# A selective scan with one product moved to GpSimd, and a Toeplitz matrix laid over 128 rows, in an eight-sublayer kernel

## The chip, the core and the metric

The kernel runs on one NeuronCore of a Trainium2 chip. Its engines are TensorE (PE; its weight loads are shown as PEld), VectorE (DVE), ScalarE (ACT), GpSimd (POOL) and SyncE (SP), which here only issues DMAs. Each engine works through its own row of instructions in order; rows wait for each other by semaphores. The metric is device time of the whole kernel in microseconds (us). A run is one execution; a time is a median of runs.

## The reference, cut to what matters

The kernel computes two layers of four sublayers each. Only two sublayers are touched. Sublayer A is a complex-valued recurrence over 2048 positions, for 2 batches, 256 channels (D) and 16 states (N):

```
c_mag(z)   = sqrt(re^2 + im^2 + 1e-8)
c_phase(z) = arctan2(im, re + 1e-10)
def step(h, inp):
    x_t, dt_t, B_t, C_t, xr_t = inp
    h_carrier = h.mean(axis=1)
    T = cos((c_phase(xr_t) - c_phase(h_carrier)) / 2) ** 2
    alpha = exp(dt_t[..., None] * A_neg)
    expo = 1 + (1 - alpha) * 0.5 * (1 - T[:, None, :])
    mag, ph = c_mag(h), c_phase(h)
    h = from_polar(min(exp(expo * log(mag + 1e-8)), 10), ph)
    h = h + B_t * (dt_t * x_t)
    h = from_polar(tanh(c_mag(h)), c_phase(h))
    y_t = einsum('bnc,bdnc->bd', C_t, h)
```

Each step needs the state of the step before, and the mean of that state over the channels. The 1e-10 in `c_phase` and the 1e-8 in `c_mag` are kept by the kernel as first-order terms.

Sublayer C, on an input of 2 x 2048 positions x 256 features:

```
x, z = split(W_in @ hidden)               # 512 channels each
x = silu(causal convolution of x with 4 taps + bias)
y = irfft(rfft(x, 2L) * rfft(k_ssm, 2L))[..., :L]   # causal, k_ssm is [512, 1024]
y = (y + x * D_skip) * silu(z)
out = W_out @ y
```

## The kernel before, in words

`tile_hybrid_kernel` (L1607) runs the sublayers one after the other: sublayer A (`scan_tables`, L159, then `scan`, L257, then an output projection), a router, sublayer B, a router, sublayer C (L1073), and then the second layer's feed-forward and attention parts (`feed_forward`, L1273, and `sublayer_d`, L1394).

**The scan.** `scan_tables` prepares, for all positions, the tables that a step needs; its `softplus` helper on VectorE ends in L254 (two SBUF tiles multiplied, 128x512), and L217 multiplies two 128x512 tiles on GpSimd. L205 copies a PSUM tile on VectorE. In `scan`, the 128 partitions are 2 batches x 16 states x 4 groups of channels, and each partition holds 64 channels (J). A state has a real and an imaginary part, so an operation that is made for both (`for k2 in range(2)`) is two instructions. `step` (L400 to L489) writes one time step; 16 steps (TG) form a group with its own tables, 32 groups form one round of the hardware loop at L514, which goes round four times: 2048 steps. Inside the loop the order of every engine's row is the order of the Python text (`manual_schedule()` at L516): no scheduler moves anything. The step goes so:

- TensorE, L410: the means `hc` and `hd` of the state, from the sums `hs` that the step before has left.
- VectorE: `gl` (L414) from `lg` of the step before, `dot` (L420), `ex` (L424) from `kd` of the step before, `ngd` (L425).
- ScalarE: `sq` (L418), `ln` (L427), `ci` (L428), `ea` = exp of `ex` (L429), `fac` (L439), and then, in `act_gap`, work for the next step or group (L391, L385).
- VectorE: `p` from the old state and `ea` (L436, L437), times `fac` (L442), plus the drive `bx` (L444), then `z`, `q`, `m2`, `r1` (L446 to L454), and `dve_gap`.
- ScalarE, L459 to L473, twelve activations that take logarithms and exponentials: `lm`, `lr`, `m`, `ir`, `e`, `rm` (inverse magnitude), `le`, `ld`, `sg`, `lb`, `k1`, `k2c`. Of these `lm`, `m`, `lr`, `le` and `lb` are PSUM tiles (`wa(...)`); the rest are in SBUF.
- VectorE, the end of the step: `p` times `ir` (L475), times e - 1 (L477), then

```
V.scalar_tensor_tensor(dl, p[:, 0], 0.5 * SMALL, rm, ALU.mult, ALU.mult)        # L480
V.tensor_tensor_reduce(out=hn[:, k2], in0=p[:, k2], in1=sg, ..., accum_out=hs)  # L482, twice
V.tensor_tensor(th, ld, le, ALU.subtract)                                       # L486
V.scalar_tensor_tensor(kc, k2c, 2.0 * MAG_EPS, k1, ALU.mult, ALU.add)           # L487
V.scalar_tensor_tensor(lg[o], th, 2.0, kc, ALU.mult, ALU.add)                   # L488
V.scalar_tensor_tensor(kd[o], kc, 0.5, dl, ALU.mult, ALU.add)                   # L489
```

L482 writes the new state into `hist` and its sum over the channels into `hs`, for which TensorE waits at L410. `dl` is the 1e-10 term (SMALL is 1e-10, MAG_EPS 1e-8). `lg`, `kd` and `hs` have two buffers each, one for odd and one for even steps. `project` (L491) multiplies the finished state with C on TensorE, one step late. GpSimd has no work in the scan. L357 and L358 make the first `kd`, once.

**Sublayer C.** 512 channels are four blocks `e` of 128; the positions are 16 blocks of 128 for each batch. The long convolution of one channel is a product with a Toeplitz matrix of its 1024 kernel values. `kernels` (L1102) loads one tile `toep` of 128 partitions x 4 x 1216: row p of it is the reversed, zero-padded kernel of a channel (`C_krev`, 1280 values to a channel) shifted by p. Each half of 64 rows belongs to four other channels, so a tile serves 8 channels. Two DMAs fill it, one issued by SyncE (r = 0) and one by ScalarE (r = 1); three buffers (`kb`). `convolve` (L1162) multiplies with it: 9 block distances `m` x 2 halves `h` x 4 channels `j` x 2 row halves `r` = 144 matmuls of 64 rows x 32 weight columns x 128 columns, into two PSUM tiles `ps[r]`, in groups that four tiles share. After four tiles `leave` (L1177) copies the two on ScalarE (L1181) and stores them to `c_yd` by ScalarE's queue.

Around this, the block `e + 1` is made and the block `e - 1` is finished in portions of 512 positions: `produce` (L1123; projection, taps of the short convolution on VectorE at L1139, SiLU `xs` on ScalarE at L1141, a store by GpSimd's queue), `turn` (L1145; 16 matmuls that transpose `xs` in halves of 64, and two copies into `xring`), `finish` (L1187; two loads by GpSimd's queue, skip and gate) and `project` (L1202; the output product). The loop at L1224 takes 16 tiles for each `e`, 64 in all, a portion every second tile. Here only TensorE's row is in the order of the text (`manual_schedule` of PE, L1120); the other rows are ordered by the scheduler. At the head of the sublayer, `norm_transpose` (L119) normalizes and transposes its input. `feed_forward` and its neighbours have no part in the change; the prediction takes the price of an instruction from L1268 (VectorE, 128x2048), L1322, L1374, L1376 and L1556 (GpSimd and VectorE products).

Of the kernel before, what the change touches and what calls it, by code (L numbers as in the profile page):

```python
# [17 lines left out]
AF = mybir.ActivationFunctionType  # L18
ALU = mybir.AluOpType
# [4 lines left out]
P = 128  # L24
B, S, D = 2, 2048, 256
NT = B * S
NI = NT // P
NB = S // P
# [9 lines left out]
SMALL = 1e-10  # L38
MAG_EPS = 1e-8
# [8 lines left out]
L_CONV = 1024  # L48
TOEP = L_CONV + P
KREV = 1280  # L50
# [3 lines left out]
HALF = P // 2  # L54
# [5 lines left out]
def new(pool, shape, name, **kw):  # L60
    return pool.tile(list(shape), F32, name=name, tag=name, **kw)


class Kernel:
# [192 lines left out]
    def scan(self, y, dtd, dxd, tabd):  # L257
# [6 lines left out]
        tc, nc = self.tc, self.nc  # L264
        V, A, G = nc.vector, nc.scalar, nc.gpsimd
        J, TURN = 64, TG * GROUPS
        with ExitStack() as c:
# [51 lines left out]
            with nc.allow_non_contiguous_dma(reason="short vectors"):  # L319
                for b in range(B):  # L320
                    rows = slice(b * 64, (b + 1) * 64)
# [78 lines left out]
            def step(k, g, before, act_gap, dve_gap):  # L400
# [61 lines left out]
                ir, e, sg, rm, ld = (w([J], n) for n in ("ir", "e", "sg", "rm", "ld"))  # L462
                A.activation(ir, lr, AF.Exp, scale=-0.5)  # L463
                A.activation(e, m, AF.Exp, scale=-2.0)
                A.activation(rm, lm, AF.Exp, scale=-1.0)
                le = wa("m")
                A.activation(le, e, AF.Ln, bias=1.0)
                A.activation(ld, e, AF.Ln, scale=-1.0, bias=1.0)
                A.activation(sg, le, AF.Exp, scale=-1.0)  # L469
                lb, k1, k2c = wa("lr"), w([J], "k1"), w([J], "k2c")  # L470
                A.activation(lb, m2, AF.Ln, bias=MAG_EPS)
                A.activation(k1, rm, AF.Ln, scale=MAG_EPS, bias=1.0)
                A.activation(k2c, lb, AF.Exp, scale=-0.5)  # L473
                for k2 in range(2):
                    V.tensor_tensor(p[:, k2], p[:, k2], ir, ALU.mult)  # L475
                for k2 in range(2):
                    V.scalar_tensor_tensor(p[:, k2], e, -1.0, p[:, k2], ALU.add, ALU.mult)  # L477
                th, kc, dl = (w([J], n) for n in ("th", "kc", "dl"))

                V.scalar_tensor_tensor(dl, p[:, 0], 0.5 * SMALL, rm, ALU.mult, ALU.mult)  # L480
                for k2 in range(2):
                    V.tensor_tensor_reduce(  # L482
                        out=hn[:, k2], in0=p[:, k2], in1=sg, scale=-1.0, scalar=0.0 if k2 else J * SMALL,
                        op0=ALU.mult, op1=ALU.add, accum_out=hs[o][:, k2 : k2 + 1],
                    )
                V.tensor_tensor(th, ld, le, ALU.subtract)  # L486
                V.scalar_tensor_tensor(kc, k2c, 2.0 * MAG_EPS, k1, ALU.mult, ALU.add)  # L487
                V.scalar_tensor_tensor(lg[o], th, 2.0, kc, ALU.mult, ALU.add)  # L488
                V.scalar_tensor_tensor(kd[o], kc, 0.5, dl, ALU.mult, ALU.add)  # L489

            def project(g, k, yps):  # L491

# [580 lines left out]
    def sublayer_c(self):  # L1073
# [11 lines left out]
        with ExitStack() as c:  # L1085
# [10 lines left out]
            xring = [new(kp, [P, HALF, 2, TAPS + NB, B], f"c_x{j}") for j in range(2)]  # L1096
            for t in xring:
                G.memset(t[:, :, :, 0:TAPS], 0.0)
# [12 lines left out]

            with tc.tile_pool(name="c_ln", bufs=2) as lp, tc.tile_pool(name="c_pl", bufs=2, space=PSUM) as pl:
# [10 lines left out]
            def produce(e, ch):  # L1123

                b, i0, cs = ch // 4, ch % 4 * 4, slice(ch * CH, (ch + 1) * CH)
                ps = new(pp, [P, CH], "ps")
                for k in range(2):
                    nc.tensor.matmul(ps, wi[:, k, e * P : (e + 1) * P], xT[:, k, cs], start=k == 0, stop=k == 1)
                xin = new(xp, [P, 3 + CH], "c_xi")
                if i0 == 0:  # L1130
                    V.memset(xin[:, 0:3], 0.0)
                else:
                    V.tensor_copy(xin[:, 0:3], last[0][:, CH : CH + 3])
                A.copy(xin[:, 3:], ps)
                last[0] = xin
                acc = new(tp, [P, CH], "c_acc")
                V.tensor_scalar(acc, xin[:, 0:CH], cw[:, e, 0:1], cb[:, e : e + 1], ALU.mult, ALU.add)
                for j in range(1, 4):
                    V.scalar_tensor_tensor(acc, xin[:, j : j + CH], cw[:, e, j : j + 1], acc, ALU.mult, ALU.add)  # L1139
                xs = new(tp, [P, CH], "c_xs")  # L1140
                A.activation(xs, acc, AF.Silu)  # L1141
                G.dma_start(out=xd[e * P : (e + 1) * P, cs], in_=xs)
                return e, ch, xs

            def turn(e, ch, xs):  # L1145

                b, i0 = ch // 4, ch % 4 * 4
                ps = new(pt, [P, 2, 4, HALF], "ps_t")
                for h in range(2):
                    for j in range(4):  # L1150
                        for r in range(2):
                            rows = slice(r * HALF, (r + 1) * HALF)
                            lo = j * P + h * HALF
                            nc.tensor.matmul(
                                ps[rows, h, j, :], xs[:, lo : lo + HALF], self.ident[:, rows], start=True, stop=True
                            )
                for h in range(2):
                    V.tensor_copy(
                        xring[e % 2][:, :, h, TAPS + i0 : TAPS + i0 + 4, b], ps[:, h].rearrange("p j c -> p c j")
                    )  # L1160

            def convolve(e, g, t, ps):  # L1162
                x = xring[e % 2]
                for m in range(TAPS + 1):
                    for h in range(2):
                        lo = L_CONV - m * P + h * HALF
                        for j in range(4):
                            for r in range(2):
                                rows = slice(r * HALF, (r + 1) * HALF)
                                nc.tensor.matmul(  # L1170
                                    ps[r][j * 32 : (j + 1) * 32, g % 4, :],
                                    x[rows, 4 * g + j, h, TAPS - m : TAPS - m + NB, :].rearrange("p i b -> p (i b)"),
                                    t[rows, j, lo : lo + P],
                                    start=m == 0 and h == 0, stop=m == TAPS and h == 1,
                                )

            def leave(e, g, ps):  # L1177

                for r in range(2):
                    ys = new(tp, [P, 4, P], "c_ys")  # L1180
                    A.copy(ys, ps[r][:, :, ::-1])  # L1181
                    rows = slice(e * P + r * HALF + 4 * g, e * P + r * HALF + 4 * g + 16)
                    A.dma_start(
                        out=yd[rows].rearrange("(s j) i b t -> (j i b) s t", j=4), in_=ys
                    )

            def finish(e, ch):  # L1187
                b, i0, cs = ch // 4, ch % 4 * 4, slice(ch * CH, (ch + 1) * CH)
# [33 lines left out]
                later(turn, t)  # L1222
            later(turn)
            for e in range(E):  # L1224
                for g in range(HALF // 4):
                    t = kernels(e, g)
                    if g % 4 == 0:
                        ps = [new(pc, [P, 4, P], f"ps_c{r}") for r in range(2)]
                    convolve(e, g, t, ps)
                    if g % 4 == 3:  # L1230
                        leave(e, g - 3, ps)
                    if g % 2 == 0:
                        work = []
                        if e + 1 < E:
                            work.append((turn, produce(e + 1, g // 2)))
                        if e > 0:
                            work.append((project, finish(e - 1, g // 2)))
# [469 lines left out]
```

## Time and profile before

| what | before |
|---|---|
| median of 3 runs | 14147.37 us (14145.97 to 14152.4) |
| the profiled execution | 14151.41 us |
| its span | 14149.7 us |
| instructions | 282029 |
| mean granted TensorE clock | 0.61 |
| busy: TensorE | 5571.1 us (39%) |
| busy: weight loads | 3830.2 us (27%) |
| busy: VectorE | 10378.9 us (73%) |
| busy: ScalarE | 8647.8 us (61%) |
| busy: GpSimd | 415.6 us (3%) |
| head of sublayer A, 0 to 310 us | GpSimd busy 24.7 us |
| the scan, 310 to 10169 us | VectorE busy 8322.7 us, ScalarE 7255.6, TensorE 2274.1, GpSimd 0 |
| sublayer C, 11095 to 12254 us | TensorE busy 694.7 us, VectorE 262.9, ScalarE 96.6; DMA share 0.70 |

How to read the profile. "Slices": the span is cut in 40 equal parts of 354 us; a digit is the busy share of an engine in tenths. "Groups": one row for a line and an engine, with the operation, out <- in by tile names, sizes, the number of instructions (x), then the busy sum in us and the mean length in ns, then the engine's idle time just before these instructions and what ended most of it. "Timeline": start in us, length in us, engine, line, operation and tiles of each instruction; lengths of instructions that follow each other overlap, so what an instruction costs its row is the spacing of starts, not its length. "Windows": a stretch, its length, the busy time and number of instructions of PE, PEld, DVE, ACT and POOL, then the granted TensorE clock, the DMA share and GB/s. "Waits": tile and line, what was waited for, then the summed us, the number of waits and the mean us of one. "Loads": a DMA's tiles, its queue, number, KB of one, and median us from issue to landing. "issue" is idle time for which the profile shows no event.

### The profile page before, as it was taken

The page shows a single profiled execution, that of the slowest core. Times are in us where ns is not written, and L with a number is a line of the kernel's source. Part 1 is how long each engine was busy: PE and PEld are TensorE (multiplying, and loading weights), DVE is VectorE, ACT ScalarE, POOL GpSimd, SP SyncE. Part 2 cuts the span into 40 slices and gives each one's busy share as a digit, 9 for nine tenths or more (in the row PEclk, how much of TensorE's full clock was granted, in tenths as well). Part 3 has the DMA queues.
Part 4 walks back from the last instruction along what each step waited for, and adds up shares of the span by engine and source line. Part 5 has one row for each costly group of instructions (what it writes and reads, how often), then busy time and mean ns, then how long its engine had stood idle before and what let it go on. Part 6 is the DMA issues. An engine that isn't in the chain of part 4 may idle for free. (4 is left out here: it accounts for less than half of the span.)

```text
span 14149.7 us, 282029 instructions
## 1 busy us (share of the span) xinstructions
PE 5571.1 (39%) x76456; PEld 3830.2 (27%) x76456; DVE 10378.9 (73%) x65267; ACT 8647.8 (61%) x44978; POOL 415.6 (3%) x496
## 2 busy tenths in 40 slices
PE   4222222222222222222222222222389655778888
PEld 2111111111111111111111111111255444544445
DVE  6888888888888888888888888888757411355555
ACT  3777777777777777777777777777535100234444
POOL 0000000000000000000000000000000000031110
PEclk6555555555555555555555555555579787889999
DMA  3000000000000000000000000000000477342220
GB/s 79 14 17 14 17 15 15 17 14 17 16 14 17 14 17 17 14 17 14 17 17 14 17 14 17 17 14 17 10 13 1 105 186 187 86 99 34 34 33 20
DMA packets 349182, 461.08 MB, mean 33 GB/s; under 512 B 205026, under 2 KB 245033, under 8 KB 346548
## 3 DMA queue, kind: packets, MB, share of 16 engines
q1 hardware_dynamic: 296372, 319.91, 10.0%
q10 hardware_dynamic: 36352, 88.61, 2.6%
q0 software_dynamic: 14848, 34.36, 0.9%
q8 instruction: 611, 10.01, 0.3%
q14 instruction: 999, 8.18, 0.2%
HBM read 385.55 MB, written 52.46 MB: 31 GB/s over the span
## 5 line engine op out<-in xcount | busy, mean ns | idle before, releaser
L410 PE MATMUL hc<-hs,mean 128*32 128x2 f32 x16384 | 588.4, 203 | 7238.6 <-DVE hs L482 7174.4
L410 PEld LDWEIGHTS hc<-hs,mean 128*32 128x32 f32 x16384 | 413.0, 140 | 7450.7 <-DVE hs L482 7386.1
L475 DVE TENSOR_TENSOR p<-p,ir 128x64 f32<-128x64 f32 x4096 | 739.6, 222 | 1063.8 <-ACT ir L463 1063.8
L494 PE MATMUL yps<-cs,hist 128*64 128x8 f32 x8192 | 1225.0, 259 | 13.4 <-DVE hs L482 13.4
L459 ACT ACTIVATE lm<-m 128x64 f32<-128x64 f32 x2048 | 466.3, 228 | 1217.1 <-DVE m L451 1217.1
L391 ACT ACTIVATE bx<-dx,tc 128x64 f32<-128x64 f32 x4098 | 1170.7, 333 | 0.1
L418 ACT ACTIVATE sq<-hc 128x2 f32<-128x2 f32 x2048 | 352.6, 172 | 1169.7 <-PE hc L410 1169.7
L1531 ACT ACTIVATE d_p<-ps_e 128x512 f32<-128x512 f32 (+3 forms) x1280 | 599.6, 537 | 755.4 <-PE ps_o L1512 532.0
L494 PEld LDWEIGHTS yps<-cs,hist 128*64 128x64 f32 x8192 | 1033.3, 218 | 45.5 <-DVE hs L482 13.8
L482 DVE CUSTOM_DVE_ANT_0 hist<-p,sg 128x64 f32<-128x64 f32 x4096 | 751.5, 220 | 11.9 <-DVE hs L482 6.0
L442 DVE TENSOR_TENSOR p<-p,fac 128x64 f32<-128x64 f32 x4096 | 741.7, 222 | 8.9 <-DVE p L437 6.5
L477 DVE SCALAR_TENSOR_TENSOR p<-e,p 128x64 f32<-128x64 f32 x4096 | 739.6, 222 | 9.9 <-ACT sg L469 9.2
L444 DVE TENSOR_TENSOR p<-p,bx 128x64 f32<-128x64 f32 x4096 | 726.9, 219 | 2.5
L439 ACT ACTIVATE fac<-ngd,ci 128x64 f32<-128x64 f32 x2048 | 712.7, 348 | 1.0 <-DVE p L436 1.0
L436 DVE SCALAR_TENSOR_TENSOR p<-hist,ea 128x64 f32<-128x64 f32 x2048 | 462.0, 226 | 323.2 <-ACT ea L429 323.2
L1524 PE MATMUL ps_e<-d_qt,d_kt 128*128 128x512 f32 (+3 forms) x1280 | 556.4, 444 | 45.7 <-ACT d_p L1531 36.4
L410 PE MATMUL hd<-hs,mean 128*32 128x2 f32 x16384 | 545.2, 193 | 0.0
L429 ACT ACTIVATE ea<-ex 128x64 f32<-128x64 f32 x2048 | 525.6, 257 | 24.4 <-DVE ex L424 5.2
L1481 PE MATMUL ps_m<-d_kt,d_qt 128*128 128x512 f32 (+3 forms) x1280 | 498.9, 436 | 98.5 <-DVE d_part L1486 38.8
L1170 PE MATMUL ps_c<-toep,c_x 64*32 64x128 f32 x18432 | 383.4, 320 | 385.2 <-issue 384.1
L432 PE MATMUL hd<-ident,ci 128*1 128x1 f32 x4096 | 386.7, 163 | 354.3 <-ACT ci L428 346.8
L1491 DVE TENSOR_REDUCE d_part<-ps_m 128x1 f32<-128x512 f32 x768 | 495.0, 684 | 41.6 <-PE ps_m L1481 40.7
(448 smaller groups left out, 22020.5 us busy)
## 6 DMA issues: line engine op xcount, KB each, us to landing
toep<-in_C_krev ACTq DMA_DIRECT2D x64, 1216.0 KB, 14.0
toep<-in_C_krev SPq DMA_DIRECT2D x64, 1216.0 KB, 9.8
ng<-dtd SPq DMA_DIRECT2D x258, 256.0 KB, 3.7
dx<-dxd SPq DMA_DIRECT2D x258, 256.0 KB, 4.2
d_kt<-d_kd SPq DMA_DIRECT2D x128, 128.0 KB, 4.3
d_qt<-d_qd SPq DMA_DIRECT2D x128, 128.0 KB, 3.9
y<-ys SPq DMA_DIRECT2D x512, 8.0 KB, 1.9
c_xd<-c_xs POOLq DMA_DIRECT2D x32, 256.0 KB, 6.6
```

Of the source, the lines that this page charges most:

```text
L391: A.activation(bx[o][:, k2], tg[j][2][:, k], AF.Identity, scale=tg[j][0][:, k2, k : k + 1], bias=0.0 if k2 else SMALL,)
L410: nc.tensor.matmul(out[r : r + 32], mean[:, r : r + 32], hs[i], start=True, stop=True)
L429: A.activation(ea, ex, AF.Exp)
L439: A.activation(fac, ngd, AF.Exp, scale=ci)
L442: V.tensor_tensor(p[:, k2], p[:, k2], fac, ALU.mult)
L444: V.tensor_tensor(p[:, k2], p[:, k2], bx[o][:, k2], ALU.add)
L475: V.tensor_tensor(p[:, k2], p[:, k2], ir, ALU.mult)
L477: V.scalar_tensor_tensor(p[:, k2], e, -1.0, p[:, k2], ALU.add, ALU.mult)
L482: V.tensor_tensor_reduce(out=hn[:, k2], in0=p[:, k2], in1=sg, scale=-1.0, scalar=0.0 if k2 else J * SMALL, op0=ALU.mult, op1=ALU.add, accu ...
L494: nc.tensor.matmul(yps[:, k, :], hist[g][:, k, k2], tg[g][3][:, k2, k], start=k2 == 0, stop=k2 == 1)
L1524: nc.tensor.matmul(s[:, q0:], ks[kt // 4][:, hh, kt % 4 * P : (kt % 4 + 1) * P], q[:, hh, q0:], start=True, stop=not diag,)
L1531: A.activation(pr[:, q0:], s[:, q0:], AF.Exp, scale=0.25)
```

## The change

In the scan, the product `dl` leaves VectorE for GpSimd and reads the new state in place of the old `p`: it no longer holds the factor 0.5e-10, and it is made after the two instructions of L482. The factor goes to the `scalar_tensor_tensor` that makes `kd`. `kd` is kept doubled, and `ex` takes half of it: a `tensor_tensor` becomes a `scalar_tensor_tensor`. The twelve activations of ScalarE get another order, in which `lb` comes sixth, `rm` eighth (ahead of `sg`), `ld` and `k1` last; `lb` gets a PSUM tile of its own.

In sublayer C, a tile `toep` now serves 4 channels, whose shifted kernels stand over all 128 rows. Row 64 + p of a channel is row p shifted by 64 further values, so only half of the tile is loaded: SyncE's DMA loads the upper 64 rows of two channels, ScalarE's the lower 64 rows of the other two (608 KB each), and the missing halves are copied on the chip, one by VectorE and one by ScalarE. `low` and `up` are the lower and the upper rows; the second two channels are held at another offset, for which `lo` makes up. There are 128 tiles instead of 64, 36 matmuls of 128 rows for each instead of 144 of 64 rows, one PSUM tile for four of them, four transposes and one copy in `turn`. A portion of `produce` and `finish` comes every fourth tile.

```
@@ scan, before the loop
-            V.scalar_tensor_tensor(n1, first[:, 0], -SMALL, n1, ALU.mult, ALU.mult)
-            V.scalar_tensor_tensor(kd[1], n2h, 0.5, n1, ALU.mult, ALU.add)
+            V.scalar_tensor_tensor(n1, first[:, 0], -2.0 * SMALL, n1, ALU.mult, ALU.mult)
+            V.tensor_tensor(kd[1], n2h, n1, ALU.add)
@@ step
-                V.tensor_tensor(ex, kd[i], gl, ALU.subtract)
+                V.scalar_tensor_tensor(ex, kd[i], 0.5, gl, ALU.mult, ALU.subtract)
...
-                A.activation(rm, lm, AF.Exp, scale=-1.0)
+                lb, k1, k2c = wa("lb"), w([J], "k1"), w([J], "k2c")
+                A.activation(lb, m2, AF.Ln, bias=MAG_EPS)
                 le = wa("m")
                 A.activation(le, e, AF.Ln, bias=1.0)
+                A.activation(rm, lm, AF.Exp, scale=-1.0)
+                A.activation(sg, le, AF.Exp, scale=-1.0)
+                A.activation(k2c, lb, AF.Exp, scale=-0.5)
                 A.activation(ld, e, AF.Ln, scale=-1.0, bias=1.0)
-                A.activation(sg, le, AF.Exp, scale=-1.0)
-                lb, k1, k2c = wa("lr"), w([J], "k1"), w([J], "k2c")
-                A.activation(lb, m2, AF.Ln, bias=MAG_EPS)
                 A.activation(k1, rm, AF.Ln, scale=MAG_EPS, bias=1.0)
-                A.activation(k2c, lb, AF.Exp, scale=-0.5)
...
-                V.scalar_tensor_tensor(dl, p[:, 0], 0.5 * SMALL, rm, ALU.mult, ALU.mult)
                 for k2 in range(2):
                     V.tensor_tensor_reduce(
...
+                G.tensor_tensor(dl, hn[:, 0], rm, ALU.mult)
                 V.tensor_tensor(th, ld, le, ALU.subtract)
                 V.scalar_tensor_tensor(kc, k2c, 2.0 * MAG_EPS, k1, ALU.mult, ALU.add)
                 V.scalar_tensor_tensor(lg[o], th, 2.0, kc, ALU.mult, ALU.add)
-                V.scalar_tensor_tensor(kd[o], kc, 0.5, dl, ALU.mult, ALU.add)
+                V.scalar_tensor_tensor(kd[o], dl, -2.0 * SMALL, kc, ALU.mult, ALU.add)
@@ sublayer_c, kernels
                 t = new(kb, [P, 4, W], "toep")
+                up, low = t[0:HALF], t[HALF:P]
                 for r in range(2):
-                    first = kr.offset + (e * P + r * HALF + 4 * g) * KREV
+                    first = kr.offset + (e * P + 4 * g + 2 * r) * KREV
                     (nc.scalar if r else nc.sync).dma_start(
-                        out=t[r * HALF : (r + 1) * HALF],
-                        in_=bass.AP(kr.tensor, first, [[1, HALF], [KREV, 4], [1, W]]),
+                        out=(low if r else up)[:, 2 * r : 2 * r + 2],
+                        in_=bass.AP(kr.tensor, first, [[1, HALF], [KREV, 2], [1, W]]),
                     )
+                V.tensor_copy(low[:, 0:2, 0 : W - HALF], up[:, 0:2, HALF:W])
+                A.copy(up[:, 2:4, HALF:W], low[:, 2:4, 0 : W - HALF])
@@ turn
+                for j in range(4):
+                    nc.tensor.transpose(ps[:, j, :], xs[:, j * P : (j + 1) * P], self.ident)
+                V.tensor_copy(
+                    xring[e % 2][:, :, TAPS + i0 : TAPS + i0 + 4, b], ps.rearrange("p j c -> p c j")
+                )
@@ convolve
+                    for j in range(4):
+                        lo = L_CONV - m * P + j // 2 * HALF
+                        nc.tensor.matmul(
+                            ps[j * 32 : (j + 1) * 32, g % 4, :],
+                            x[:, 4 * g + j, TAPS - m : TAPS - m + NB, :].rearrange("p i b -> p (i b)"),
+                            t[:, j, lo : lo + P], start=m == 0, stop=m == TAPS,
+                        )
@@ leave
+                ys = new(tp, [P, 4, P], "c_ys")
+                A.copy(ys, ps[:, :, ::-1])
+                rows = slice(e * P + 4 * g, e * P + 4 * g + 16)
+                A.dma_start(out=yd[rows].rearrange("(s j) i b t -> (j i b) s t", j=4), in_=ys)
@@ the loop
-                for g in range(HALF // 4):
+                for g in range(P // 4):
...
-                    if g % 2 == 0:
+                    if g % 4 == 0:
...
-                    else:
+                    elif g % 4 == 2:
```

More of the change, by code (lines that the diff above doesn't have):

```diff
@@ L1095, in sublayer_c @@
             dk = self.load_cols(kp, "C_D_skip")
-            xring = [new(kp, [P, HALF, 2, TAPS + NB, B], f"c_x{j}") for j in range(2)]
+            xring = [new(kp, [P, P, TAPS + NB, B], f"c_x{j}") for j in range(2)]
             for t in xring:
-                G.memset(t[:, :, :, 0:TAPS], 0.0)
+                G.memset(t[:, :, 0:TAPS], 0.0)
             kb = c.enter_context(tc.tile_pool(name="c_kb", bufs=3))
@@ L1147, in turn @@
                 b, i0 = ch // 4, ch % 4 * 4
[L1148 to L1160, printed above, removed]
+                ps = new(pt, [P, 4, P], "ps_t")
+                for j in range(4):
[3 more added lines that the diff above has]
+                )
             def convolve(e, g, t, ps):
@@ L1164, in convolve @@
                 for m in range(TAPS + 1):
[L1165 to L1175, printed above, removed]
-            def leave(e, g, ps):
[L1179 to L1185, printed above, removed]
+                    for j in range(4):
[5 more added lines that the diff above has]
+                        )
+            def leave(e, g, ps):
+                ys = new(tp, [P, 4, P], "c_ys")
+                A.copy(ys, ps[:, :, ::-1])
+                rows = slice(e * P + 4 * g, e * P + 4 * g + 16)
+                A.dma_start(out=yd[rows].rearrange("(s j) i b t -> (j i b) s t", j=4), in_=ys)
             def finish(e, ch):
@@ L1224, in sublayer_c @@
             for e in range(E):
-                for g in range(HALF // 4):
+                for g in range(P // 4):
                     t = kernels(e, g)
                     if g % 4 == 0:
-                        ps = [new(pc, [P, 4, P], f"ps_c{r}") for r in range(2)]
+                        ps = new(pc, [P, 4, P], "ps_c")
                     convolve(e, g, t, ps)
@@ L1231, in sublayer_c @@
                         leave(e, g - 3, ps)
-                    if g % 2 == 0:
+                    if g % 4 == 0:
                         work = []
                         if e + 1 < E:
-                            work.append((turn, produce(e + 1, g // 2)))
+                            work.append((turn, produce(e + 1, g // 4)))
                         if e > 0:
-                            work.append((project, finish(e - 1, g // 2)))
-                    else:
+                            work.append((project, finish(e - 1, g // 4)))
+                    elif g % 4 == 2:
                         for f, args in work:
```

## The prediction, made before the changed kernel was run

> **What bounds the kernel now.** I read the page first (engine rows by slice, costliest groups), then VectorE's timeline over one step of the scan, then the waits, windows and loads of the Toeplitz stage.
>
> ```profile
> DVE  6888888888888888888888888888757411355555
> DMA  3000000000000000000000000000000477342220
> L410 PE MATMUL hc<-hs,mean 128*32 128x2 f32 x16384 | 588.4, 203 | 7238.6 <-DVE hs L482 7174.4
> L475 DVE TENSOR_TENSOR p<-p,ir 128x64 f32<-128x64 f32 x4096 | 739.6, 222 | 1063.8 <-ACT ir L463 1063.8
> ```
>
> Slices 2 to 28 look alike: the 2048 dependent scan steps, from 363.6 us (first L414) to 10175.2 us (last L489), so 4.79 us each. TensorE idles for the sums of L482, VectorE for L463: no engine is full, and a step is one loop of dependences, mostly VectorE's. The Toeplitz loop runs from 11171.0 to 12170.2 us, where the DMA digit is 7. One step's end on VectorE (start, length):
>
> ```profile
> 5007.05 0.36 DVE L477 SCALAR_TENSOR_TENSOR p<-e,p 128x64 f32<-128x64 f32 x2
> 5007.38 0.23 DVE L480 SCALAR_TENSOR_TENSOR dl<-p,rm 128x64 f32<-128x64 f32 x1
> 5007.53 0.22 DVE L482 CUSTOM_DVE_ANT_0 hist<-p,sg 128x64 f32<-128x64 f32 x1
> 5007.67 0.08 DVE L482 DVE_READ_ACCUMULATOR2_ANT hs<- 128x1 f32 x1
> 5007.67 0.22 DVE L482 CUSTOM_DVE_ANT_0 hist<-p,sg 128x64 f32<-128x64 f32 x1
> ...
> 5007.81 0.22 DVE L486 TENSOR_TENSOR th<-ld,m 128x64 f32<-128x64 f32 x1
> 5007.95 0.22 DVE L487 SCALAR_TENSOR_TENSOR kc<-k2c,k 128x64 f32<-128x64 f32 x1
> 5008.20 0.23 DVE L488 SCALAR_TENSOR_TENSOR lg<-th,kc 128x64 f32<-128x64 f32 x1
> 5008.34 0.22 DVE L489 SCALAR_TENSOR_TENSOR kd<-kc,dl 128x64 f32<-128x64 f32 x1
> ```
>
> There is no gap from L480 to L489, and the chain runs on through gl, ex, ngd (L414 to L425) to ScalarE's exponentials. So dl costs the step its whole spacing, 0.143 us (0.15 in this rounding).
>
> **The scan, part by part.** Count from the first hist of a step, T0.
>
> Gain: without dl on VectorE, hist follows L477. It also needs sg. ScalarE keeps sg ninth in its row, so sg still ends at 7.35 in this step; dl starts at 7.38, and hist can start there. Everything behind it moves up 0.143 us: 2048 x 0.143 = 293 us.
>
> ScalarE's new order: ld and k1 now come last, k2c earlier. Logarithms follow each other at 0.15 us and exponentials at 0.11, so k1, last, ends near 7.75, and ld near 7.60. th would start at 7.67 and kc at 7.81: no wait, with some 0.05 us to spare. Were a tenth of a microsecond missing, it would cost 205 us; I take nothing. lb now has its own PSUM tile: nothing. rm's new wait is on a GpSimd product two steps old: nothing. L424 and L489 keep one VectorE instruction each (226 and 218 ns before; scalar_tensor_tensor rows cost 218 to 226): nothing. L357/L358 run once.
>
> Added: dl on GpSimd, and kd's wait for it. The trace has no such product in the scan; its nearest rows (mean ns behind the comma):
>
> ```profile
> L1556 POOL TENSOR_TENSOR d_on<-d_on,d_rc 128x512 f32<-128x512 f32 x32 | 40.9, 1277 | 65.5 <-DMA d_rc<-d_sd 65.5
> L1322 POOL TENSOR_TENSOR d_half<-d_rot,d_half 128x1024 fp32r<-128x1024 f32 x16 | 37.9, 2370 | 18.5 <-ACT d_half L1321 17.3 <-DMA d_qd<-d_half 1.2
> L217 POOL TENSOR_TENSOR sa_dx<-sa_dt,sa_xin 128x512 f32<-128x512 f32 x16 | 22.8, 1422 | 266.9 <-DVE sa_dt L255 266.9
> ```
>
> From 1277 and 2370 a line of 2.13 ns an element over 0.18 us: 64 elements take 0.32 us. hist's accumulator read ends at T0+0.23; GpSimd starts 0.08 us after VectorE's end where it waits for it (L1376 behind L1374, six times 79 to 87 ns). So dl runs from T0+0.31 to T0+0.63. kd stood at T0+0.81: its own wait is covered by 0.15 us.
>
> But L217 shows two lengths, 1.27 and 1.58 us, and its neighbour on VectorE stretches with it:
>
> ```profile
> 79.71 1.58 POOL L217 TENSOR_TENSOR sa_dx<-sa_dt,sa_xin 128x512 f32<-128x512 f32 x1 [22.00 <-DVE sa_dt L255]
> 80.20 1.64 DVE L254 SCALAR_TENSOR_TENSOR sp_a<-sp_a,sp_s 128x512 f32<-128x512 f32 x1
> ```
>
> L254 takes 0.69 us alone (its fastest eight), 1.16 or 1.64 beside L217: it really starts at 81.84 - 0.69 = 81.15, 0.14 us before L217's end at 81.29. L205 and L1374, with one input in PSUM, do not stretch. kc (L487) reads two SBUF tiles and would start at T0+0.42; th reads one from PSUM. By this row kc may start at T0+0.63-0.14 = 0.49, 0.065 us late, and lg, kd, gl, ex, ngd queue behind it. Net 0.143 - 0.065 = 0.078 us a step, 160 us. The Trainium skill ("SBUF — State Buffer", section "SBUF: two separate sides") is harsher: a VectorE instruction with two SBUF inputs and a reading GpSimd instruction hold the shared port pair exclusively, and the loser blocks for the whole instruction. Then kc waits until 0.63, 0.21 us late, and the step grows by 0.06 us: +130 us. The row is of this chip and of this pair of instructions, so I take the row. Ends: 0 late (-293 us) to 0.21 late (+130 us).
>
> **The Toeplitz stage.** Views: windows, waits, loads.
>
> ```profile
> 11171.00:12171.00 1000.00, 596.72 (x19579) 450.73 (x19580) 151.17 (x262) 60.20 (x103) 45.23 (x74) 0.80 0.75 182
> PE ps_c L1170 <- issue: 384.1, 86, 6.7
> toep<-in_C_krev ACTq DMA_DIRECT2D x64, 1216.0 KB, 14.0
> toep<-in_C_krev SPq DMA_DIRECT2D x64, 1216.0 KB, 9.8
> ```
>
> DMA share is 0.75 at 182 GB/s; TensorE waits 384 us for "issue", in stalls of about 6 us, not for data. Each tile's two loads start when TensorE has finished a tile (11357.18, 11372.42), they move one after the other (9.8 and 14.0 us to land), and while they move TensorE, after some 160 records at 16 ns, waits for more instructions. One tile (8 channels) takes 15.6 us, 16 channels 31.2 us.
>
> Removed: half the matmuls (18432 records to 9216), so half their instructions; the 6 us stalls should mostly go. Not removed: bytes. 128 tiles with two loads of 608 KB are the same 159 MB, whose floor at 182/0.75 = 243 GB/s is 656 us. Added: 128 copies of 2304 elements on each of VectorE and ScalarE. VectorE: 128x2048 in 1.27 us (L1268), so 1.4 us, beside idle time. ScalarE: 0.22 us at 64 and 0.59 at 512 elements, so 2.1 us. That copy stands in the queue that issues half of the loads. In the built program ScalarE's row over four tiles is: load 9, ys copy, load 10, ys store, xi copy, copy 9, (silu), copy 10, xs, load 11, load 12, copy 11, copy 12. Each copy holds up the next load; before, loads only waited for a buffer.
>
> Chain, from the end of copy 8: the packet records give 1.4 us from issue to the first packet, 2.8 us for 608 KB (2.49 MB in 11 us before) and 1.0 us to the semaphore, in order of arrival. Load 9 lands at 5.2; SP's 10 at 8.0; ScalarE's 10, issued at 1.2 behind ys, at 10.8; SP's 11 at 13.6. Copy 9 ends at 7.6, copy 10 at 12.9. xs waits for VectorE's taps (L1139), queued behind its copy 11: it ends at 17.7. Loads 11 and 12 follow, land at 23.4 and 26.2; copy 12 ends at 28.3. For e = 0 load 11 precedes xs: 26.9. The x and y traffic, 1 MB per 16 channels, is 4.6 us of DMA; I let half fall into idle time: 30 us, 32 x 30 = 960 against 999, -39 us. The first copies in the layer norm wait for the first loads, +5 us. So -35 us.
>
> This takes 2.5 us for a tile's 72 full-row records (32 ns each, as many rows a second as before). The skill speaks against it ("TensorE: Matmul & The Clock Gate", Part 3): a weight load hides under running matmuls only in another row group, and full-row tiles have none. With 0.107 us (the LDWEIGHTS row) laid bare in each of 18 rounds of four, a tile takes 4.2 us; three places of the chain depend on it, +5 us: 35 us, 1120 us, +120. Lower end: 27 us if all other traffic is hidden, -136. No run here shows full-row loads of this shape; I stay at 30, since TensorE has slack over most of the chain.
>
> **Sum.** The profiled execution is 14151.4 us (span 14149.7), 4 us over the median, 14147.4: 14147 - 160 - 35 = 13952, said as 13950.
>
> **Rivals.**
> 1. The port costs nothing (GpSimd has read its 64 elements before kc asks): -293, and -100 in the stage as other traffic hides: 13755. For it: 64 elements are few. Against: eight of eight L254 beside L217 stretched.
> 2. The change moves work without gaining: hist's second half also delays dl by its 0.08 us (L217's 1.58), kc is 0.145 late and eats the 0.143; the stage stays at its pace, because the ScalarE queue takes the place of the instruction stalls. About 14130.
> 3. Slower: GpSimd holds the port until dl's end. Place L487, price 0.21 us a step, +130, with -35 from the stage 14240. The scan loses from the point at which kc is over 0.143 us late, that is dl's release after T0+0.565; I put the release at 0.49.
>
> **Chances.** Forecast 0.48 (13850 to 14020), rival 1 0.20, rival 2 0.20, rival 3 0.12. The range 13720 to 14150 leaves out rival 3 and a little below rival 1. A measurement can tell about 0.2% (28 us) from no change: faster 0.76 (forecast, rival 1, part of 2), same 0.11, slower 0.13.
>
> **What would show it.** Steps of 4.71 us instead of 4.79; hist at sg's end; L487 with a length of 0.28 instead of 0.22 us, or a later start; GpSimd's dl at 0.32 us; no wait of L489 for GpSimd. In the stage: "issue" waits well under 384 us, ScalarE's copies near 2.1 us, a loop of 960 us. Wrong if dl lasts over 0.4 us, if th or kc wait for ScalarE, or if the loop falls below 860 us or exceeds 1050.

## The result, and the profile after

The changed kernel takes 13973.03 us (13969.83 to 13977.73, 4 runs) against 14148.51 us (14145.97 to 14152.4, 4 runs) before: a ratio of 0.9876, 95% interval 0.9859 to 0.9893, or -175 us. The forecast was 13950, -197 from the 14147 that it started from. The profiled executions, 14151.41 and 13969.83 us, with spans of 14149.7 and 13968.1, split at five instants: the starts of the first and the last `gl` (L414), of the first `toep` load and of the first Toeplitz matmul, and the end of the last one.

| stretch | before, us | after, us | difference |
|---|---|---|---|
| head, to the first gl | 363.6 | 365.0 | +1.4 |
| scan, first to last gl | 9807.0 | 9731.3 | -75.7 |
| last gl to first toep load | 924.5 | 929.8 | +5.3 |
| first toep load to first Toeplitz matmul | 75.9 | 78.5 | +2.6 |
| Toeplitz loop | 999.5 | 887.7 | -111.8 |
| the rest | 1979.2 | 1975.8 | -3.4 |

So the sum was nearly right, and neither term was: the scan gave half of the 160 us forecast, the Toeplitz stage three times its 35. That the two errors, 84 us one way and 74 the other, nearly cancel is luck. A step takes 4.752 us before and 4.720 after at the median (4.791 and 4.754 on average).

The groups and loads of the page after (busy sum, mean ns; KB of one load, us to landing):

```profile
L484 POOL TENSOR_TENSOR dl<-hist,rm 128x64 f32<-128x64 f32 x2048 | 653.4, 319 | 9145.8 <-DVE hs L480 9145.8
...
L486 DVE SCALAR_TENSOR_TENSOR kc<-k2c,k 128x64 f32<-128x64 f32 x2048 | 575.5, 281 | 1.4
...
toep<-in_C_krev ACTq DMA_DIRECT2D x128, 608.0 KB, 8.6
toep<-in_C_krev SPq DMA_DIRECT2D x128, 608.0 KB, 8.7
```

GpSimd's `dl` takes 0.319 us (0.32 had been worked out), and `kc`, 218 ns before, takes 281: two of the signs that the prediction had named. Of its other signs, the copies on ScalarE (2.11 us, 2.1 worked out) and the end of TensorE's issue waits came true; the step (4.754 us on average, 4.71 forecast), the start of hist and the length of the loop did not. The row of `kc` before:

```profile
L487 DVE SCALAR_TENSOR_TENSOR kc<-k2c,k 128x64 f32<-128x64 f32 x2048 | 447.1, 218 | 0.1
```

The timeline of one step's end, over all engines (start, length):

```profile
5024.87 0.36 DVE L477 SCALAR_TENSOR_TENSOR p<-e,p 128x64 f32<-128x64 f32 x2
5024.92 0.22 ACT L470 ACTIVATE sg<-m 128x64 f32<-128x64 f32 x1
...
5025.24 0.23 DVE L480 CUSTOM_DVE_ANT_0 hist<-p,sg 128x64 f32<-128x64 f32 x1
...
5025.54 0.22 DVE L485 TENSOR_TENSOR th<-ld,m 128x64 f32<-128x64 f32 x1
5025.55 0.32 POOL L484 TENSOR_TENSOR dl<-hist,rm 128x64 f32<-128x64 f32 x1 [4.40 <-DVE hs L480]
5025.67 0.28 DVE L486 SCALAR_TENSOR_TENSOR kc<-k2c,k 128x64 f32<-128x64 f32 x1
5025.99 0.22 DVE L487 SCALAR_TENSOR_TENSOR lg<-th,kc 128x64 f32<-128x64 f32 x1
...
5026.13 0.22 DVE L488 SCALAR_TENSOR_TENSOR kd<-dl,kc 128x64 f32<-128x64 f32 x1
```

Two things are to be seen. `hist` starts 0.37 us after L477; before, `dl` started 0.33 after L477 and `hist` 0.48. So hist moved up by 0.11 and not by 0.143. And `kc` ends at 5025.95, late by 0.066 against its usual length, with `lg` behind it; `kd` follows `lg` at its usual 0.14, so it does not wait for GpSimd.

The windows of the Toeplitz loop by block of 128 channels, first before, then after (length, then busy PE, PEld, DVE, ACT, POOL; granted clock, DMA share, GB/s):

```profile
11171.00:11404.00 233.00, 132.94 (x4896) 104.05 (x4896) 28.66 (x57) 14.03 (x24) 4.34 (x8) 0.77 0.76 179
11404.00:11672.00 268.00, 163.70 (x4991) 122.58 (x4992) 50.15 (x88) 18.84 (x32) 14.72 (x24) 0.82 0.76 185
11672.00:11937.00 265.00, 162.21 (x5010) 120.12 (x5017) 50.63 (x88) 18.84 (x32) 15.76 (x26) 0.81 0.76 185
11937.00:12170.00 233.00, 136.87 (x4683) 103.22 (x4673) 21.74 (x31) 8.01 (x14) 10.40 (x16) 0.77 0.74 177
```

```profile
11105.00:11301.00 196.00, 119.41 (x2368) 91.38 (x2360) 68.50 (x78) 73.59 (x52) 4.32 (x8) 0.82 0.94 212
11301.00:11545.00 244.00, 159.41 (x2458) 112.92 (x2462) 95.08 (x114) 86.84 (x65) 17.93 (x24) 0.79 0.85 202
11545.00:11787.00 242.00, 158.58 (x2481) 112.29 (x2476) 93.62 (x111) 85.07 (x64) 17.62 (x26) 0.79 0.86 203
11787.00:11992.00 205.00, 137.20 (x2402) 102.47 (x2396) 63.47 (x62) 73.77 (x47) 14.42 (x16) 0.81 0.96 216
```

The inner two blocks take 30.4 us for 16 channels (243/8); 30 was forecast. The outer two take 24.6 and 25.7, at a DMA share of 0.94 to 0.96. And TensorE's largest wait of the loop, "issue: 384.1" at L1170 before (86 stalls of 4.5 us on average), is now another, with 1.1 us of issue waits left at this line:

```profile
PE ps_c L1162 <- ACT toep L1111: 185.6, 95, 6.3
```

ScalarE's row in the second block shows what is behind it: two loads are issued only when the SiLU `xs` is through, and ScalarE then waits for their data and copies.

```profile
11320.34 0.63 ACT L1143 ACTIVATE c_xs<-c_acc 128x512 f32<-128x512 f32 x1 [2.31 <-DVE c_acc L1141]
11320.35 1.62 ACTq L1106 DMA_DIRECT2D toep<-in_C_krev  x2
11333.48 4.32 ACT L1111 COPY toep<-toep 64x2304 f32<-64x2304 f32 x2 [12.51 <-DMA toep<-in_C_krev]
```

### The profile page after: what moved, and what is told of

The parts are those of the page before. It is cut to its first block, busy times and chain, and to the rows that moved or that the text cites. A ratio compares the mean times of both kernels' runs of the same rounds, so it can differ in the third digit from the quotient of the medians.

```text
span 13968.1 us, 262793 instructions
## 1 busy us (share of the span) xinstructions
PE 5544.9 (40%) x66344; PEld 3795.2 (27%) x66344; DVE 10459.2 (75%) x63315; ACT 8855.0 (63%) x45106; POOL 1077.3 (8%) x2544
## 5 line engine op out<-in xcount | busy, mean ns | idle before, releaser
L475 DVE TENSOR_TENSOR p<-p,ir 128x64 f32<-128x64 f32 x4096 | 739.3, 222 | 1065.1 <-ACT ir L463 1065.1
L484 POOL TENSOR_TENSOR dl<-hist,rm 128x64 f32<-128x64 f32 x2048 | 653.4, 319 | 9145.8 <-DVE hs L480 9145.8
L493 PEld LDWEIGHTS yps<-cs,hist 128*64 128x64 f32 x8192 | 1033.2, 218 | 45.3 <-DVE hs L480 13.7
L442 DVE TENSOR_TENSOR p<-p,fac 128x64 f32<-128x64 f32 x4096 | 742.3, 222 | 9.0 <-DVE p L437 5.3
L477 DVE SCALAR_TENSOR_TENSOR p<-e,p 128x64 f32<-128x64 f32 x4096 | 741.7, 223 | 8.0 <-ACT sg L470 5.3
L486 DVE SCALAR_TENSOR_TENSOR kc<-k2c,k 128x64 f32<-128x64 f32 x2048 | 575.5, 281 | 1.4
```

What stands on the lines that cost most here:

```text
L442: V.tensor_tensor(p[:, k2], p[:, k2], fac, ALU.mult)
L484: G.tensor_tensor(dl, hn[:, 0], rm, ALU.mult)
L493: nc.tensor.matmul(yps[:, k, :], hist[g][:, k, k2], tg[g][3][:, k2, k], start=k2 == 0, stop=k2 == 1)
```

## The experiments

The kernel before was measured anew beside each group of runs (14138 to 14150 us). Where a run is set against the changed kernel, that kernel's time is taken as 0.9876 of the kernel before beside it.

**The two parts alone.** `scan_only` is the changed kernel with the old `sublayer_c`; `toep_only` the kernel before with the new one.

> The scan of the changed kernel with the sublayer C of before. The two traces put 76 us of the 175 on the scan (from the first gl to the last) and 109 on the stretch from the first toep load to the last Toeplitz matmul. Theory, the two parts are independent: 14148 - 76 = 14072, steps of 4.72 us at the median. Rival, one part shifts what the other finds (loads and instruction fetches): more than 20 us away from that.

> The sublayer C of the changed kernel with the scan of before. Theory, independent parts: 14148 - 105 = 14043, Toeplitz loop near 888 us, steps of 4.75 us. The prediction's own size of this part was -35: 14113. Rival, the parts are not independent: this run and scan_only together do not add up to -175 within 20 us.

Measured: scan_only 14066.77 us against 14139.05 (ratio 0.9947, interval 0.9931 to 0.9964), -72; toep_only 14033.77 (0.9926, 0.9909 to 0.9943), -105. Together -177, against -175: the parts add up. The loop takes 887.6 us in toep_only, the step 4.715 in scan_only. Both sizes differ from the forecast's, so each needs a cause of its own.

**ScalarE's order alone.** On the kernel before:

```
+lb = wa("lb")                     # was wa("lr"), after sg
-rm, le, ld, sg, lb, k1, k2c       # order of the activations
+lb, le, rm, sg, k2c, ld, k1
```

> The kernel before with ScalarE's new order of the twelve activations and lb's own PSUM tile, and nothing else. Theory (the prediction's): nothing, 14148 within 15 us, steps of 4.75 us, since dl waits for VectorE's p and not for sg, and th and kc find ld and k1 ready. Rival: the order alone brings part of the scan's gain, 20 us or more (sg ends 0.03 us earlier), or costs (k1 ends 0.07 us later).

Measured: 14137.69 us against 14139.05, ratio 1.0001 (0.9992 to 1.001); steps of 4.744 us. The order by itself is worth nothing, as forecast. That it matters in company shows below.

**dl left out.**

```
-G.tensor_tensor(dl, hn[:, 0], rm, ALU.mult)
...
-V.scalar_tensor_tensor(kd[o], dl, -2.0 * SMALL, kc, ALU.mult, ALU.add)
+V.scalar_tensor_tensor(kd[o], kc, 1.0, kc, ALU.mult, ALU.max)
```

> The changed kernel without dl: kd is kc alone, so the 1e-10 term of the phase is left out; VectorE still spends one instruction on kd. Theory: kc alone pays for GpSimd's product, 0.066 us a step; it returns to 0.218 us and the step to 4.654: 13973 - 135 = 13838. Rival 1, kc is long for another reason (ScalarE's or TensorE's accesses): 13973, kc still 0.28 us. Rival 2, GpSimd's product delays more than kc (hist's second half, th, kd's wait): 13800 or less.

Measured: 13828.24 us (ratio 0.9781, 0.9764 to 0.9797), -135 against the changed kernel. `kc` is back at 218 ns, the step at 4.648. GpSimd's product costs those 0.07 us a step, and no more.

**kc with an input in PSUM.** SBUF and PSUM are the two on-chip memories that tiles stand in. GpSimd's product stays, and `k2c` is written to `lb`'s PSUM tile:

```
-A.activation(k2c, lb, AF.Exp, scale=-0.5)
+A.activation(lb, lb, AF.Exp, scale=-0.5)
...
-V.scalar_tensor_tensor(kc, k2c, 2.0 * MAG_EPS, k1, ALU.mult, ALU.add)
+V.scalar_tensor_tensor(kc, lb, 2.0 * MAG_EPS, k1, ALU.mult, ALU.add)
```

> The changed kernel with k2c written in place into lb's PSUM tile, so that kc reads one SBUF tile and one PSUM tile; GpSimd's dl stays. Theory, kc is held by GpSimd because both read SBUF on two inputs: kc returns to 0.218 us, the step to 4.654, 13973 - 135 = 13838. Rival, kc is held by dl in any case: kc 0.28 us, 13973. In between, if lg (th and kc, both in SBUF) takes the place of kc: lg starts when kc ends and dl still runs 0.07 us at most beyond the lock's end, so at most 0.01 us a step is lost again.

Measured: 13831.43 us (0.9785, 0.9768 to 0.9801), -132. Two of its groups:

```profile
L484 POOL TENSOR_TENSOR dl<-hist,rm 128x64 f32<-128x64 f32 x2048 | 652.9, 319 | 9000.1 <-DVE hs L480 9000.1
...
L486 DVE SCALAR_TENSOR_TENSOR kc<-lb,k 128x64 f32<-128x64 f32 x2048 | 442.1, 216 | 1.4
```

dl takes as long as in the changed kernel and lies in the same place (4.00 to 4.32 us after gl; kc starts at 4.12), and kc is not held. So GpSimd's product stretches kc only where kc reads two SBUF inputs beside it.

**sg one place earlier, then one later.** In the changed kernel, sg ahead of rm:

```
-A.activation(rm, lm, AF.Exp, scale=-1.0)
 A.activation(sg, le, AF.Exp, scale=-1.0)
+A.activation(rm, lm, AF.Exp, scale=-1.0)
```

> The changed kernel with sg one place earlier in ScalarE's row, ahead of rm. hist starts 0.143 us after the first product of L477 ends and 0.100 us after sg ends. Theory, sg sets it: sg ends 0.11 us earlier, hist moves up by 0.038 to the place where dl stood, 13973 - 78 = 13895. Rival, the accumulating instruction itself starts 0.04 us later than a plain one behind a wait: no change, 13973, hist 0.21 us after sg's end. Third, hist gains less because the second product of L477 stands 0.14 us ahead of it in the row: also no change.

Measured: 14091.61 us (0.9971, 0.9961 to 0.9981), 128 slower than the changed kernel, which no theory had said. sg did not end earlier (3.590 us after gl, 3.593 in the changed kernel): it follows le, and rm had only filled the gap between the two, so the question put was not tested. But dl started 0.062 us later, 4.069 instead of 4.007 us after gl, and kc grew with it (groups of sg_first):

```profile
L486 DVE SCALAR_TENSOR_TENSOR kc<-k2c,k 128x64 f32<-128x64 f32 x2048 | 670.2, 327 | 1.2
...
L484 POOL TENSOR_TENSOR dl<-hist,rm 128x64 f32<-128x64 f32 x2048 | 659.3, 322 | 9268.1 <-DVE hs L480 9125.3 <-ACT ld L472 142.8
```

In the changed kernel dl carries a single wait, for VectorE: hist has waited for sg, and rm stands ahead of sg in ScalarE's row, so rm is done as well. With rm behind sg, GpSimd has to wait for ScalarE too; the trace then shows a semaphore instruction of its own in GpSimd's row ahead of each dl (number; shortest, median and longest ns; first and last start), which the changed kernel does not have:

```profile
L484 POOLq EVENT_SEMAPHORE  x2048: 17/17/17, 369.6 to 10226.6; - x187
```

dl comes 0.06 us later although rm has ended long before (3.705). So the place of rm, ahead of sg, is worth these 128 us. The run also gives a second point on how long kc is held: kc ends 0.079 us after dl's end here, 0.082 in the changed kernel.

```
-A.activation(sg, le, AF.Exp, scale=-1.0)
 A.activation(k2c, lb, AF.Exp, scale=-0.5)
+A.activation(sg, le, AF.Exp, scale=-1.0)
```

> The changed kernel with sg one place later in ScalarE's row, behind k2c. In sg_first sg could not end earlier, because it follows le directly; so the question what sets hist's start is asked the other way. sg will end about 0.115 us later (3.71 us after gl instead of 3.59). Theory, sg sets hist's start with 0.100 us between: hist moves by the full 0.115, 13973 + 236 = 14209. Rival, the accumulating instruction starts 0.143 us behind VectorE's own product by itself and sg has slack (other ScalarE results are taken up 0.033 us after their end): hist moves by 0.05 only, 13973 + 105 = 14078.

Measured: 14053.13 us (14049.14 to 14084.23; ratio 0.9931, 0.9915 to 0.9948), 78 slower than the changed kernel; the profiled execution is the longest of the four. In it:

```profile
5021.17 0.36 DVE L477 SCALAR_TENSOR_TENSOR p<-e,p 128x64 f32<-128x64 f32 x2
...
5021.33 0.23 ACT L471 ACTIVATE sg<-m 128x64 f32<-128x64 f32 x1
...
5021.59 0.22 DVE L480 CUSTOM_DVE_ANT_0 hist<-p,sg 128x64 f32<-128x64 f32 x1
```

sg ends 0.124 us later (3.717 after gl), hist starts 0.055 later, 0.03 after sg. In the changed kernel it starts 0.10 after sg. So there sg has slack, and hist's start is its own: 0.143 us behind the end of L477's first product, where `dl`, a plain instruction behind the same product, started 0.104 behind it. Three facts narrow the cause. L442 and L477, plain instructions that wait in the same way, start 0.104 us behind the product ahead of them too. The number of waits is the same, for dl of before and hist of after both wait for VectorE and for ScalarE, and both have a semaphore instruction ahead of them (first before, then after):

```profile
L480 DVEq EVENT_SEMAPHORE  x2048: 21/21/21, 368.6 to 10174.2; - x187
L480 DVEq EVENT_SEMAPHORE  x2048: 21/21/21, 370.1 to 10099.9; - x187
```

And where ScalarE's result comes last, as in sg_late, hist starts as soon behind it (0.03 us) as a plain instruction does (L475 behind ir, 0.033). So it is the kind of the instruction, behind VectorE's own product; whether its accumulator or something else in it is the reason was not tried.

**Both loads from SyncE.**

```
-(nc.scalar if r else nc.sync).dma_start(
+nc.sync.dma_start(
```

> The changed kernel with both loads of a tile issued by SyncE, so that no copy on ScalarE holds a load up. The loop takes 197, 244, 241 and 205 us for the four blocks; the outer two at a DMA share of 0.94 to 0.96, the inner two at 0.85. Theory of the prediction (ScalarE's row holds the loads): the inner blocks fall towards 205 to 215 us each, together -60, 13913. Rival 1, three buffers and the copies set the pace: no change within 15 us. Rival 2, the loads now wait behind each other on SyncE's row for two buffers: slower.

Measured: 13890.63 us (0.9825, 0.9808 to 0.9841), -72. The blocks take 184, 215, 214 and 212 us, the loop 825, and its window shows

```profile
11091.00:11916.00 825.00, 550.00 (x9697) 406.07 (x9698) 321.36 (x364) 323.60 (x229) 60.26 (x74) 0.84 0.97 224
```

The inner blocks fall to 215: ScalarE's row had held the loads. The last block, which has no xs, gains nothing (205 us in the changed kernel). Now DMA is busy for 0.97 of the loop.

**What the loop of before waited for.** Two kernels made from the one before:

```
# half_mm: half of the matmuls
-for h in range(2):
+for h in range(1):
...
# half_loads: half of the bytes, the same matmuls
-t = new(kb, [P, 4, W], "toep"); ... [[1, HALF], [KREV, 4], [1, W]]; ... t[rows, j, lo : lo + P]
+t = new(kb, [P, 2, W], "toep"); ... [[1, HALF], [KREV, 2], [1, W]]; ... t[rows, j // 2, lo : lo + P]
```

> The kernel before with half of the Toeplitz matmuls left out (only the products of h = 0), loads unchanged: its outputs lack half of the long convolution. It asks what held the loop of before at 15.6 us a tile. Theory, the instruction fetches behind the load bursts: with half the instructions the 384 us of issue waits at the Toeplitz matmuls fall to under 150, and the loop from 999 to about 890, as in the changed kernel: 14148 - 110 = 14040. Rival, the loads and the buffers' turnover set the pace: loop within 20 us of 999, 14140.

> The kernel before with half of the Toeplitz bytes: each load brings two channels instead of four (608 KB), and the matmuls of the other two use the same rows, so half of the channels are convolved with a wrong kernel; all 144 matmuls of a tile stay. With half_mm it asks whether TensorE's issue stalls come from the instructions alone or from instructions that wait behind load bursts. Theory, behind bursts: the stalls of about 6 us shrink with the burst, the 384 us of issue waits fall to under 150, the loop from 999 to 650 to 750 us: about 13850. Rival, the fetches take as long by themselves: loop within 30 us of 999, 14120.

Measured: half_mm 13833.17 us (0.9786, 0.977 to 0.9802), -305; half_loads 13976.68 (0.988, 0.9864 to 0.9897), -174. TensorE's wait at the Toeplitz matmuls, then the loop's window, first of half_mm:

```profile
PE ps_c L1170 <- issue: 87.4, 35, 6.4
```

```profile
11157.00:11854.00 697.00, 439.78 (x10361) 302.18 (x10362) 150.78 (x263) 59.72 (x103) 45.08 (x74) 0.73 0.97 259
```

and of half_loads:

```profile
PE ps_c L1170 <- issue: 250.3, 83, 5.8
```

```profile
11168.00:11991.00 823.00, 550.28 (x19571) 418.03 (x19575) 151.39 (x263) 59.73 (x102) 45.10 (x74) 0.86 0.53 129
```

With half the instructions the issue waits at the Toeplitz matmuls fall from 384 us to 87 (those of all of TensorE's lines from 385 to 140) and the loop to 697, where the DMA share is 0.97 (TensorE's own busy time falls too, from 597 us to 440); the expectation had the direction, and a third of the size. With half the bytes there are as many stalls as before (83 against 86), but of 3.0 us instead of 4.5 on average, and the loop takes 823 us at a DMA share of 0.53. So the stalls belong to the number of instructions, and the bursts make each longer. For half_loads both figures of the expectation missed (waits under 150 us, a loop of 650 to 750): the stalls are long even beside half the bytes. Of the 176 us by which its loop is shorter, these stalls make up some 134; most of the rest is busy time of TensorE, 46 us less at a granted clock of 0.86 instead of 0.80.

That TensorE waits there for its own instructions can be read from the DMA packets. The profile has a DMA queue named "instruction", with packets of 16384 bytes. Of the 75 stalls over 1.5 us in the loop of before, four in five end 1.3 to 1.6 us after such a packet has ended; four in five instants taken at random lie 0.7 to 8.3 us after one.

**The gains together.** `best` is kc_psum and loads_sp in one; `best_v` makes both copies of a tile on VectorE besides (`A.copy` becomes `V.tensor_copy`).

> kc_psum and loads_sp together: k2c in PSUM, both loads of a tile issued by SyncE. The gains lie in different stages: 13973 - 142 - 82 = 13749. Rival: they share something and add up to less by over 20 us.

> As best, with both copies of a tile on VectorE (1.36 us there, 2.11 us on ScalarE). In loads_sp TensorE waits 193 us for ScalarE's copies, but the DMA share of its loop is 0.93 to 1.00. Theory, the loads are the bound now: within 15 us of best. Rival, the copy is on the chain: 0.75 us for each tile and more, over 50 us faster; or VectorE's taps and copies queue behind each other: over 15 us slower.

Measured: best 13768.64 us against 14150.28 before, ratio 0.973 (0.9713 to 0.9746), and 206 us under the changed kernel; the two single gains were 132 and 72, together 204. It is the fastest kernel here. best_v takes 13820.39 (0.9766, 0.975 to 0.9782), 52 more: its last block grows from 212 us to 243. That is the last of the three cases named; that VectorE's row holds the block was not shown by itself.

## Why the prediction was right in the sum and wrong in its terms

**"dl starts at 7.38, and hist can start there": the step that failed in the scan.** It gave hist the whole 0.143 us of dl's spacing. hist gained 0.105 (3.798 to 3.693 us after gl), because it starts 0.143 us behind the product that it now waits for, and the plain dl whose place it took 0.104: 0.038 us x 2048 = 78 us of the 84 that are missing. sg, which the prediction had checked, was not the limit (sg_late). 0.008 us more, 16 us, went into a wider spacing from hist to th. Stalls off this pattern fell by 10 us. With the forecast's terms so replaced: -293 + 78 + 135 + 16 - 10 = -74, and 76 were measured.

**kc held by GpSimd: right, in mechanism and size.** 0.065 us was said, 0.066 measured, and kc_psum and no_dl both give it back. Of the measured row and the skill's rule the row was right: held to dl's end, kc would have ended 0.218 after it; it ends 0.082 after it, so it runs from 0.136 us before dl's end on, as L254 did beside L217 (0.14). Rival 3, which took the rule's full hold, and rival 1, which took none, are both excluded. So is rival 2's delay of dl by hist's second half: dl starts 0.314 us after hist and lasts 0.319, as forecast. The other half of what the Trainium skill says there ("SBUF — State Buffer", section "SBUF: two separate sides"), that the conflict takes two SBUF inputs on VectorE, holds: with one in PSUM it is gone.

**kd's wait covered, th and kc in time: right.** The claim on ScalarE's order, "nothing", was right for VectorE and for the order alone, but the step treated rm's wait and not dl's: it did not see that rm ahead of sg spares GpSimd a second wait. The forecast of dl's start (hist's read end + 0.08) was right only because the change has that order, which is luck.

**The Toeplitz stage: "30 us, 32 x 30 = 960", the step that failed.** The stalls went, as forecast, although the prediction read one as about 6 us (4.5 on average; 6.7 is the longest). The chain by load, copy and ScalarE's row gave 30 us for 16 channels where 30.4 were measured. In two rounds of the second block, xs ended 13.7 and 19.4 us after copy 8 (17.7 forecast) and copy 12 ended 30.5 and 31.1 us after it, so the chain is the right one, though single links were off. But it was worked out for a block that makes the next one and finishes the last one, and then used for all four; the 26.9 us that the prediction itself had for the first block's chain, instead of 28.3, did not enter the sum. The first block has no `finish` and so less traffic; the last has no `produce`, so no xs to wait for in ScalarE's row, and less traffic too: 24.6 and 25.7 us, together 8 x (5.4 + 4.3) = 78 us under the forecast, which is more than all of the 72 us between 960 and 888. These two causes are read from the traces; that the last block gained nothing in loads_sp fits the second, and no run took a `finish` or a `produce` away by itself. A sign was there: the windows before show blocks of 233, 268, 265 and 233. The start cost 2.6 us, not 5.

**Full-row weight loads: they stay hidden.** A tile's 36 matmuls run in 2.15 us where nothing is waited for (tile 2: first start 11112.74, last end 11114.89). The prediction said 2.5 (its own 72 records of 32 ns are 2.3), and 4.2 with the loads laid bare by the rule that it quoted against itself: on this shape the measurement goes against that rule.

**Where the rest of the stage's gain went.** Halving the instructions alone took the loop to 697 us; the changed kernel, with as few, is at 888. ScalarE's row accounts for 63 of the 191 us (loads_sp, 825). The other 128 remain at a DMA share of 0.97, and there the open point is that the same share moves 224 GB/s with the copies and 259 in half_mm. A packet of 4864 bytes takes 0.341 us on average in loads_sp and 0.293 in half_mm; but it takes 0.327 in the loop of before and 0.344 in half_loads, where there are no copies either, so the copies alone do not explain it. What makes the transfers slower was not tried.

## What to carry to other kernels

When an instruction leaves a chain, the gain is set by the start of what takes its place, not by the spacing of what left: look up how long each kind of instruction starts behind what it waits for. Work moved to GpSimd costs VectorE where two SBUF inputs meet it, so put one of them in PSUM, and order the producers so that GpSimd needs one wait. A loop that overlaps neighbours has other first and last rounds: work the chain out for each, and when a stage's instructions stall, count instructions before bytes.

## What the runs showed of the hardware

- An accumulating VectorE instruction (`tensor_tensor_reduce`) started 0.143 us behind the end of the VectorE product it waits for, plain ones 0.104 (L442, L477, dl).
- A second semaphore to wait for delayed GpSimd's product by 0.06 us, although rm, the one it waited for, had ended over 0.3 us before.
- A VectorE instruction with two SBUF inputs, held by a GpSimd product, went on 0.136 to 0.14 us ahead of that product's recorded end, in three places (L254, and kc in the changed kernel and in sg_first); with one input in PSUM it was not held (kc 216 ns).
- DMA shares of 0.97 meant 224 GB/s in one loop and 259 in another.
- With 18432 records of matmuls in the loop TensorE stood 385 us for its instructions, with 9216 of the same form 140 us; half the bytes of data left as many stalls, each shorter (3.0 us instead of 4.5).
